# Statistics pass of a four-layer convolution kernel: scaling moved to GpSimd, loads into eight shared buffers

## The chip, the cores and the metric

The kernel runs on one core of a Trainium2 chip. The metric is the device time of one execution in microseconds (us); less is better. A core has five engines that run in parallel, each with its own queue of instructions: TensorE (PE in the profile), VectorE (DVE), ScalarE (ACT), GpSimd (POOL) and SyncE (SP, which here only issues DMA transfers). Engines wait for each other through semaphores.

## The reference

The input `x` has shape (4, 16, 512, 512). Four layers follow each other, each on all of it:

- layer 0: a depthwise 3x3 convolution, attention in windows of 8x8, and an MLP with GELU;
- layer 1: fake quantisation of the input and of the weights, a 3x3 convolution, a batch norm over the whole batch, and a clip to 0..6;
- layer 2: two 3x3 convolutions with a ReLU between them, and a residual;
- layer 3: a 3x3 convolution, a pointwise MLP of 128 hidden channels, and a residual.

What matters here is layer 1:

```python
def _fake_quant(v, n_bits, scaling_range):
    qp = float(2 ** (n_bits - 1) - 1)
    alpha = scaling_range * jnp.max(jnp.abs(v))
    step = alpha / qp
    q = jnp.clip(jnp.round(v / step), -qp, qp) * step
    return v + jax.lax.stop_gradient(q - v)

xq = _fake_quant(x, N_BITS_A, SCALE_RANGE_IN)
wq = _fake_quant(weight, N_BITS_W, 1.0)
y = conv(xq, wq)                        # 3x3, same size
mean = jnp.mean(y, axis=(0, 2, 3))
var = jnp.var(y, axis=(0, 2, 3))
inv = gamma * jax.lax.rsqrt(var + BN_EPS)
y = y * inv + (beta - mean * inv)
return jnp.clip(y, 0.0, ACT_THRES)
```

The mean and the variance run over the whole output of the convolution. They must be known before the first value of layer 1 can be finished.

## The kernel before

The program has three stages. The first, `window_attention`, computes layer 0 and writes its result to a DRAM buffer `x1` of 65 blocks, each of 128 partitions x 4 x 512 float32 values (1 MB). It also collects the largest absolute values in `peak`. The other two are in `conv_layers`: a **statistics pass**, which computes layer 1's convolution for its mean and variance only and keeps none of its values, and then the **layer pass**, which reads `x1` again and computes layers 1, 2 and 3 together in one long pipeline (the loop `for t in range(-2, M + 7)`).

The statistics pass takes one block per step, 64 steps (M is 64). Per step:

- `load` brings a block from `x1` into an SBUF tile `tx` by one DMA of 1 MB, issued by SP. The pass has four tiles, two of the tag "x" and two of the tag "o" in the pool `ld`, in turn. Each is written again once ScalarE has read it. `load` runs four steps ahead.
- `scaled` (L984) multiplies the tile by 1/step and adds the constant `ROUND`, in place, on VectorE: 128 partitions x 2048 float32 values. The addition rounds to integers.
- `rounded` (L987) takes the constant off again on ScalarE and writes bfloat16 into the inner columns of a tile of the ring `q` (three tiles, 514 columns wide, of which the two outer columns are zero). `scaled` and `rounded` run two steps ahead of the convolution.
- `_conv_turn` (L908) is called 24 times with four matmuls each: 96 matmuls of 32x32 weights on 512 columns, into four PSUM banks of 512 values. Odd and even steps use different sets of four banks.
- `bn_stats` (L1009) reads each of the four banks on VectorE and leaves six values a partition.

Ahead of the loop, `quant_step` finds the maximum over `peak`; a GpSimd instruction takes it over the partitions. Behind the loop, two more tiles (-2 and -1, for the rows outside the blocks) are loaded, scaled and rounded, `bn_aggr` (L1031) puts the statistics together, and some twenty instructions on one column turn them into `scale` and `shift`.

The order of PE's, VectorE's, ScalarE's and SP's instructions in `conv_layers` is the order of the program (`manual_schedule`). GpSimd's instructions are placed by the compiler's scheduler.

The layer pass has rings of its own for what goes from layer to layer: `z` (3 tiles), `h` (2), `x` (2), `xi` (3) and `y` (3). All are 128 x 4 x 514 float32 values, and all have zeros in their two outer columns, which `ring` (L947) writes on GpSimd. None of these five rings is used in the statistics pass.

Of the kernel before, what the change touches and what calls it, by code (L numbers as in the profile page):

```python
# [11 lines left out]
F32 = mybir.dt.float32  # L12
BF16 = mybir.dt.bfloat16
AF = mybir.ActivationFunctionType
ALU = mybir.AluOpType
# [8 lines left out]
B, C, H, W = 4, 16, 512, 512  # L24
P = 128
HR = H // 2
WP = W + 2
NS = 8
S = 4
M = H // S // 2  # L30
# [5 lines left out]
ROUND = 12582912.0  # L36
# [77 lines left out]
def conv_chain(ctx: ExitStack, tc: tile.TileContext, x, xw, mats, vecs, cqs, cws, hots, out):  # L114
# [32 lines left out]
    with tc.If(safe == 0):  # L147
        attention_block(tc, x, x1, m, v, peak)
    conv_layers(tc, x1, out, cw, cq, sw, m, v, peak)


# [700 lines left out]
def quant_step(nc, pool, out, columns, name):  # L852

    most = pool.tile([P, 1], F32, name=f"most_{name}")
    nc.vector.tensor_reduce(most, columns, AX.X, ALU.max, apply_absolute_value=True)
    every = pool.tile([P, 1], F32, name=f"every_{name}")
    nc.gpsimd.partition_all_reduce(every, most, P, bass_isa.ReduceOp.max)
    step = out.tile([P, 1], F32, name=f"step_{name}")
    nc.vector.tensor_scalar(step, every, 1.0 / QP, None, ALU.mult)
    inv = out.tile([P, 1], F32, name=f"inv_{name}")  # L860
    nc.vector.reciprocal(inv, step)
    return step, inv
# [21 lines left out]
def _load_pairs(nc, t, x1, mm):  # L884


    if mm < 0:
        nc.vector.memset(t[:, 0], 0.0)
        nc.sync.dma_start(t[:, 1:S], x1[M + mm, :, 0 : S - 1])
    elif mm < M:  # L890
        nc.sync.dma_start(t, x1[mm])
    else:
        nc.sync.dma_start(t[:, 0 : S - 1], x1[mm - M, :, 1:S])
        if mm == M:
            nc.sync.dma_start(t[:, S - 1], x1[M, :, S - 1])
        else:
            nc.vector.memset(t[:, S - 1], 0.0)


def _turns():  # L900

    return [(side, dx, i) for side in range(2) for dx in range(3) for i in range(4)]


def _conv_turn(nc, p, weights, src, side, dx, i):

    for j in range(4):
        nc.tensor.matmul(  # L908
            p[i][_quad(j)], weights[_quad(i), side, dx, :],
            src[side][_quad(i), j, dx : dx + W],  # L910
            start=side == 0 and dx == 0, stop=side == 1 and dx == 2,
        )
# [3 lines left out]
def conv_layers(ctx: ExitStack, tc, x1, out, cw, cq, sw, m, v, peak):  # L916
# [18 lines left out]
    nc = tc.nc  # L935
    ld = ctx.enter_context(tc.tile_pool(name="l3l", bufs=2))
    act = ctx.enter_context(tc.tile_pool(name="l3a", bufs=1))
# [2 lines left out]
    banks = [ps.tile([P, W], F32, name=f"tb{i}") for i in range(8)]  # L940
    conv_banks, hid_banks = banks[0:4], banks[4:8]

    def ring(name, n, dt=F32):
        tiles = []
        for i in range(n):
            t = act.tile([P, 4, WP], dt, name=f"{name}{i}")
            nc.gpsimd.memset(t[:, :, 0 : WP : WP - 1], 0.0)  # L947
            tiles.append(t)
        return lambda mm: tiles[mm % n]

    qs = ring("q", 3, BF16)
    zs, hs, xs, xi, ys = ring("z", 3), ring("h", 2), ring("x", 2), ring("xi", 3), ring("y", 3)

    edge_b1 = act.tile([P, 2], F32, name="edge_b1")
    nc.vector.tensor_scalar(edge_b1, v("edge"), v("l2_b1"), None, ALU.mult)
# [19 lines left out]

    loaded = {}

    def load(mm, tag="x"):
        loaded[mm] = ld.tile([P, S, W], F32, tag=tag, name=f"tx{mm}")
        _load_pairs(nc, loaded[mm], x1, mm)  # L980

    def scaled(mm, at=slice(0, S)):
        t = loaded[mm][:, at]
        nc.vector.tensor_scalar(t, t, ix, ROUND, ALU.mult, ALU.add)  # L984

    def rounded(mm, at=slice(0, S)):
        nc.scalar.activation(  # L987
            inner(qs(mm))[:, at], loaded[mm][:, at], AF.Identity, bias=unround
        )


    tags = ("x", "o")
    for mm in range(4):
        load(mm, tags[mm % 2])
    sx, ix = quant_step(nc, act, act, peak, "x")
    for mm in range(2):
        scaled(mm)
        rounded(mm)
    for mm in range(M):
        if mm + 4 <= M:  # L1000
            load(mm + 4, tags[mm % 2])
        if mm + 2 <= M:
            scaled(mm + 2)
            rounded(mm + 2)
        p = banks[4 * (mm % 2) : 4 * (mm % 2) + 4]
        for turn in _turns():
            _conv_turn(nc, p, cq, (qs(mm), qs(mm + 1)), *turn)
        for b in range(B):
            nc.vector.bn_stats(stats[:, mm * B + b, :], p[b])  # L1009
    for mm in (-2, -1):  # L1010
        load(mm)
        scaled(mm)
        rounded(mm)
# [11 lines left out]
    def mul(a, b, name):  # L1025
        t = act.tile([P, 1], F32, name=f"mul_{name}")
        nc.vector.tensor_tensor(t, a, b, ALU.mult)
        return t
# [9 lines left out]
    s = mul(sx, sw, "s")  # L1038
# [135 lines left out]
    for t in range(-2, M + 7):  # L1174
# [5 lines left out]
        mm = t - 4  # L1180
# [5 lines left out]
        mm = t - 3  # L1186
# [7 lines left out]
        mm = t - 1  # L1194
# [4 lines left out]
        mm = t  # L1199
# [135 lines left out]
```

## Time and profile before

| | us |
|---|---|
| runs | 6492.53, 6498.27, 6499.6 |
| median | 6498.27 |
| profiled execution | 6499.56 |
| its span, first to last instruction | 6497.8 |
| statistics pass, first to last block of statistics (L1009), starts | 3573.7 to 3804.7 |
| PE busy in the span | 6264.0 (96%) |
| ACT busy | 4179.7 (64%) |
| DVE busy | 3186.5 (49%) |
| POOL busy | 6.0 (0%) |

The profile is of one execution. In its 40 slices of equal length each digit is the busy share of a slice in tenths. "PEclk" is the clock that TensorE was granted, as a share of full speed. In the groups of instructions a line names the code line, engine, operation, what is written and read, and the count, and behind the bar the busy time in us, the mean of one in ns, and the idle time of the engine just before with what ended it. In the timeline a line begins with start and length in us, and the bracket is the idle time before it and what ended it. Times of instructions that overlap on an engine are counted once in busy times.

### The profile page before, as it was taken

How to read it: one execution, taken by the hardware profiler on the slowest of the kernel's cores; microseconds unless marked ns; L12 is line 12 of the kernel's file. 1: busy time of each engine (PE TensorE's matmuls, PEld its weight loads, DVE VectorE, ACT ScalarE, POOL GpSimd, SP SyncE). 2: the span in 40 equal slices, each digit the busy share in tenths (PEclk: the TensorE clock that was granted, in tenths of full speed). 3: DMA queues.
4: the chain of work that ended last, by engine and by line, in shares of the span. 5: the costliest groups of instructions: out<-in, count | busy, mean ns of one | idle time of the engine just before them, and what ended most of it. 6: DMA issues, size and time to landing. Idle time of an engine off the chain costs nothing. (4 is left out here: it accounts for less than half of the span.)

```text
span 6497.8 us, 317055 instructions
## 1 busy us (share of the span) xinstructions
PE 6264.0 (96%) x146976; PEld 3402.1 (52%) x146976; DVE 3186.5 (49%) x4640; ACT 4179.7 (64%) x5738; POOL 6.0 (0%) x26
## 2 busy tenths in 40 slices
PE   8999999999999999999997669999999999999999
PEld 5555555555555555555553335455555554555553
DVE  3444444444444444444443974544445554545554
ACT  5777777777777777777775544555555555555554
POOL 0000000000000000000000000000000000000000
PEclk9999999999999999999997879999999999999999
DMA  3333333333333333333322842222222222222221
GB/s 82 62 71 62 71 63 70 63 70 63 70 63 70 63 70 62 71 61 72 60 56 61 298 161 75 81 82 86 83 82 81 82 83 82 84 83 81 81 65 48
DMA packets 544390, 515.30 MB, mean 79 GB/s; under 512 B 349008, under 2 KB 480208, under 8 KB 514384
## 3 DMA queue, kind: packets, MB, share of 16 engines
q1 hardware_dynamic: 542768, 494.52, 29.2%
q8 instruction: 1154, 18.91, 1.2%
q14 instruction: 180, 1.47, 0.1%
q10 hardware_dynamic: 288, 0.39, 0.0%
HBM read 225.87 MB, written 134.48 MB: 55 GB/s over the span
## 5 line engine op out<-in xcount | busy, mean ns | idle before, releaser
L1123 ACT ACTIVATE hid<-tb,vec 128x512 f32<-128x512 f32 x1280 | 847.5, 687 | 1127.8 <-PE tb L1117 1126.5
L1117 PE MATMUL tb<-y,mat 32*32 32x512 f32 x16384 | 1567.9, 599 | 2.0 <-DVE o L1139 1.3
L367 ACT ACTIVATE e<-pair 128x1024 f32<-128x1024 f32 x1024 | 992.3, 1021 | 225.0 <-PE pair L359 224.3
L1125 DVE TENSOR_SCALAR hid<-tb,vec 128x512 f32<-128x512 f32 x768 | 575.3, 749 | 890.0 <-PE tb L1117 872.8
L295 PE MATMUL pair<-x,taps 32*32 32x512 f32 x18432 | 965.8, 605 | 1.9 <-ACT y L306 1.3
L416 PE MATMUL bank<-y,fc_e 32*32 32x512 f32 x8192 | 878.4, 607 | 3.7 <-ACT hid L421 3.2
L421 ACT ACTIVATE hid<-bank,f1b 128x512 f32<-128x512 f32 x1024 | 679.6, 686 | 298.8 <-PE bank L416 285.3
L351 DVE COPY yt<-bank 128x512 f32<-128x512 f32 x512 | 353.8, 691 | 906.1 <-PE bank L346 905.8
L359 PE MATMUL pair<-g,y 32*128 32x128 f32 x16384 | 651.2, 285 | 40.4 <-ACT e L367 39.3
L1117 PEld LDWEIGHTS tb<-y,mat 32*32 32x32 f32 x16384 | 496.4, 103 | 329.4 <-issue 185.0
L908 PE MATMUL tb<-z,cw 32*32 32x512 f32 x12864 | 640.4, 603 | 4.2 <-ACT z L1054 3.4
L359 PEld LDWEIGHTS pair<-g,y 32*128 32x128 f32 x16384 | 540.2, 186 | 186.8 <-ACT e L367 109.2
L908 PE MATMUL tb<-x,cw 32*32 32x512 f32 x12480 | 620.0, 597 | 1.5 <-ACT z L1054 1.5
L295 PEld LDWEIGHTS pair<-x,taps 32*32 32x32 f32 x18432 | 459.3, 103 | 286.3 <-issue 182.9
L908 PE MATMUL tb<-h,cw 32*32 32x512 f32 x12672 | 590.7, 601 | 1.8 <-ACT z L1054 1.5
L378 PE MATMUL bank<-e,yt 128*32 128x128 f32 x16384 | 555.3, 276 | 0.9 <-ACT r L393 0.9
L908 PE MATMUL tb<-q,cq 32*32 32x512 bf16 x12672 | 418.5, 424 | 138.4 <-ACT q L987 103.2
L383 PE MATMUL bank<-e,hot 128*32 128x512 f32 x4096 | 535.0, 593 | 0.0
L378 PEld LDWEIGHTS bank<-e,yt 128*32 128x32 f32 x16384 | 417.6, 109 | 108.1 <-DVE yt L351 52.8
L1133 PE MATMUL tb<-hid,mat 128*32 128x512 f32 x4096 | 471.1, 601 | 0.0
L429 DVE TENSOR_TENSOR xo<-bank,y 128x512 f32<-128x512 f32 x256 | 177.1, 692 | 547.2 <-PE bank L427 545.5
L346 PEld LDWEIGHTS bank<-mat,y 128*128 128x128 f32 x2048 | 215.3, 141 | 431.7 <-issue 378.1
(150 smaller groups left out, 6661.2 us busy)
## 6 DMA issues: line engine op xcount, KB each, us to landing
tx<-x SPq DMA_DIRECT2D x128, 1024.0 KB
x<-in_xw_dram SPq DMA_DIRECT2D x32, 2600.0 KB
y<-y SPq DMA_DIRECT2D x2048, 32.0 KB
xi<-x SPq DMA_DIRECT2D x1024, 64.0 KB
out_dram<-o SPq DMA_DIRECT2D x64, 1024.0 KB
x<-xo SPq DMA_DIRECT2D x2000, 32.0 KB
tx<-x SPq DMA_DIRECT2D x4, 768.0 KB
x<-xo SPq DMA_DIRECT2D x48, 24.0 KB
```

The lines of the kernel that those rows point to most:

```text
L295: nc.tensor.matmul(bank(u)[quad(vv)], taps[quad(u), tap, :], xts[n // 2][quad(u), vv, dy : dy + WS, at : at + BW], start=tap == 0, stop=ta ...
L359: nc.tensor.matmul(bank(u)[:, P * jj : P * jj + P], y2[quad(u), vv, jl + jj].rearrange("p w t -> p (w t)"), g[quad(u), vv, jl + jj].rearra ...
L367: nc.scalar.activation(e[:, 2 * i : 2 * i + 2].rearrange("p u j t -> p u (j t)"), pairs[i], AF.Exp,)
L378: nc.tensor.matmul(b[quad(u), P * jj : P * jj + P], yt[:, jj, quad(u)], e[:, u, jj, :], start=True, stop=True,)
L383: nc.tensor.matmul(d[quad(u)], own, e[:, u].rearrange("p j t -> p (j t)"), start=True, stop=True,)
L416: nc.tensor.matmul(b[quad(k)], fc1[quad(vv), quad(k)], y[quad(vv), u, :], start=True, stop=True,)
L421: nc.scalar.activation(hd, b, AF.Gelu, bias=f1b)
L908: nc.tensor.matmul(p[i][_quad(j)], weights[_quad(i), side, dx, :], src[side][_quad(i), j, dx : dx + W], start=side == 0 and dx == 0, stop= ...
L1117: nc.tensor.matmul(p[_quad(c)], w1[_quad(b), 1 - par, 32 * c : 32 * c + 32], inner(ys(mm + par))[_quad(b), s, :], start=True, stop=True,)
L1123: nc.scalar.activation(hd, p, AF.Relu, bias=v("l3_b1"))
L1125: nc.vector.tensor_scalar(hd, p, v("l3_b1"), 0.0, ALU.add, ALU.max)
L1133: nc.tensor.matmul(p[_quad(b), :], w2[:, par], hd, start=par == 0, stop=par == 1)
```

## The change

The loop's scalings go from VectorE to GpSimd (`scaled` takes an engine). The scalings of tiles 0 and 1, those of tiles -2 and -1, and those of the layer pass stay on VectorE. The pass's loads no longer use tiles of the pool `ld`. They go into the eight tiles of the rings `y`, `xi` and `x`, seen as flat rows of which the first 2048 of 2056 values are used. The loads run eight steps ahead, and a step's load stands behind its statistics in the program. The zeros in the outer columns of these three rings are written behind the loop, since the loads overwrite some of them; those of `q`, `z` and `h` stay where they were.

```diff
+    rings = {}
+
     def ring(name, n, dt=F32):
-        tiles = []
-        for i in range(n):
-            t = act.tile([P, 4, WP], dt, name=f"{name}{i}")
+        tiles = rings[name] = [
+            act.tile([P, 4, WP], dt, name=f"{name}{i}") for i in range(n)
+        ]
+        return lambda mm: tiles[mm % n]
+
+    def border(name):
+        for t in rings[name]:
             nc.gpsimd.memset(t[:, :, 0 : WP : WP - 1], 0.0)
-            tiles.append(t)
-        return lambda mm: tiles[mm % n]
 
     qs = ring("q", 3, BF16)
     zs, hs, xs, xi, ys = ring("z", 3), ring("h", 2), ring("x", 2), ring("xi", 3), ring("y", 3)
+    for name in "qzh":
+        border(name)
...
-    def load(mm, tag="x"):
-        loaded[mm] = ld.tile([P, S, W], F32, tag=tag, name=f"tx{mm}")
+    def load(mm, t=None):
+        if t is None:
+            t = ld.tile([P, S, W], F32, tag="x", name=f"tx{mm}")
+        loaded[mm] = t
         _load_pairs(nc, loaded[mm], x1, mm)
 
-    def scaled(mm, at=slice(0, S)):
+    def scaled(mm, at=slice(0, S), engine=nc.vector):
         t = loaded[mm][:, at]
-        nc.vector.tensor_scalar(t, t, ix, ROUND, ALU.mult, ALU.add)
+        engine.tensor_scalar(t, t, ix, ROUND, ALU.mult, ALU.add)
...
-    tags = ("x", "o")
-    for mm in range(4):
-        load(mm, tags[mm % 2])
+
+    flat = [
+        t.rearrange("p s x -> p (s x)")[:, 0 : S * W].rearrange("p (s x) -> p s x", x=W)
+        for t in rings["y"] + rings["xi"] + rings["x"]
+    ]
+    AHEAD = len(flat)
+    for mm in range(AHEAD):
+        load(mm, flat[mm])
     sx, ix = quant_step(nc, act, act, peak, "x")
     for mm in range(2):
         scaled(mm)
         rounded(mm)
     for mm in range(M):
-        if mm + 4 <= M:
-            load(mm + 4, tags[mm % 2])
         if mm + 2 <= M:
-            scaled(mm + 2)
+            scaled(mm + 2, engine=nc.gpsimd)
             rounded(mm + 2)
         p = banks[4 * (mm % 2) : 4 * (mm % 2) + 4]
         for turn in _turns():
             _conv_turn(nc, p, cq, (qs(mm), qs(mm + 1)), *turn)
         for b in range(B):
             nc.vector.bn_stats(stats[:, mm * B + b, :], p[b])
+        if mm + AHEAD <= M:
+            load(mm + AHEAD, flat[mm % AHEAD])
+    for name in ("x", "xi", "y"):
+        border(name)
```

## The prediction

> **What bounds the kernel now.** I read the page's 40 slices first. They show one short stretch unlike the rest: around slice 22 VectorE (DVE) and the DMA engines rise and TensorE (PE) falls.
>
> ```profile
> PE   8999999999999999999997669999999999999999
> DVE  3444444444444444444443974544445554545554
> POOL 0000000000000000000000000000000000000000
> DMA  3333333333333333333322842222222222222221
> ```
>
> That is the statistics pass. Everywhere else PE is the bound and the change touches nothing there, so the rest of the reading is of this pass. The table of windows gives its busy times (us, PE busy, PEld busy, DVE, ACT, POOL, PE clock, DMA share, GB/s):
>
> ```profile
> 3563.00:3566.00 3.00, 0.00 (x0) 0.00 (x0) 0.00 (x0) 0.00 (x0) 0.00 (x0) 0.50 0.90 371
> 3566.00:3569.00 3.00, 0.00 (x0) 0.00 (x0) 1.52 (x2) 1.25 (x1) 0.00 (x0) 0.50 1.04 437
> ...
> 3575.00:3800.00 225.00, 136.06 (x5952) 83.29 (x5936) 223.18 (x311) 122.98 (x62) 0.00 (x0) 0.83 0.80 288
> ```
>
> DVE is busy 223.18 of 225 us. No other engine is above 136, GpSimd (POOL) does nothing, and the loads run at 288 GB/s where the first ones reached 437. The groups of instructions inside this window say what DVE does:
>
> ```profile
> L1009 DVE BATCH_NORM_STATS2 stats<-tb 128x6 f32<-128x512 f32 x249 | 154.7, 682 | 1.8 <-PE tb L908 0.8
> L908 PE MATMUL tb<-q,cq 32*32 32x512 bf16 x5952 | 136.7, 459 | 88.9 <-ACT q L987 66.0 <-issue 22.1
> L987 ACT ACTIVATE q<-tx,unround 128x2048 bf16<-128x2048 f32 x62 | 124.3, 2005 | 102.4 <-DVE tx L984 72.3 <-PE tb L908 30.0
> L984 DVE TENSOR_SCALAR tx<-tx,inv_x 128x2048 f32<-128x2048 f32 x62 | 78.6, 1268 | 0.0
> ```
>
> Per step of the pass DVE does four statistics and one scaling, and never waits to speak of (1.8 us). ScalarE (ACT) waits for the scaling, PE waits for ACT: both are followers. The timeline of DVE shows the beat:
>
> ```profile
> 3692.88 1.27 DVE L984 TENSOR_SCALAR tx<-tx,inv_x 128x2048 f32<-128x2048 f32 x1
> 3694.07 2.48 DVE L1009 BATCH_NORM_STATS2 stats<-tb 128x6 f32<-128x512 f32 x4
> 3696.47 1.27 DVE L984 TENSOR_SCALAR tx<-tx,inv_x 128x2048 f32<-128x2048 f32 x1
> ```
>
> Start to start the scaling costs 3694.07 - 3692.88 = 1.19 us and the four statistics 3696.47 - 3694.07 = 2.40 us: 3.59 us a step. From the first group of statistics (3573.71) to the 64th (3802.87) there are 63 steps in 229.16 us, 3.637 us each. That is the figure to beat.
>
> [...] The trace of before has no elementwise GpSimd instruction with an input; it only has a fill:
>
> ```profile
> L279 POOL MEMSET y<- 128x4096 f32 x1 | 3.5, 3518 | 0.0
> ```
>
> 3518 ns for 4096 elements is 0.86 ns an element: [...]reading isn't shown. [...]
>
> **The change part by part.**
>
> 1. Off DVE: 63 scalings of 1.19 us each (those of tiles 0 and 1, before the loop, and the two after it stay). The DVE beat falls from 3.59 to 2.40 us. This is a gain only down to the next limit.
>
> 2. What is late next, per step. ACT's rounding: 2.00 us. PE: one timeline entry has 96 matmuls in 1.66 us at full clock; at half clock (right after the pass) 96 take 2.79 us. The clock was 0.83 on average at 60% busy[...]. Loads: 1.0486 MB at 437 GB/s is 2.40 us, and the first tiles landed 2.38 and 2.49 us apart:
>
> ```profile
> 3566.38 1.28 DVE L984 TENSOR_SCALAR tx<-tx,inv_x 128x2048 f32<-128x2048 f32 x1 [3.51 <-DMA tx<-x]
> 3568.76 1.29 DVE L984 TENSOR_SCALAR tx<-tx,inv_x 128x2048 f32<-128x2048 f32 x1 [1.09 <-DMA tx<-x]
> 3571.25 1.29 DVE L984 TENSOR_SCALAR tx<-tx,inv_x 128x2048 f32<-128x2048 f32 x1 [1.21 <-DMA tx<-x]
> ```
>
> So 2.44 us if the rate lasts. The other bound comes from the steady stretch: 288 GB/s at a share of 0.80 scales to 360 GB/s, or 2.91 us. I take 2.44, because a rate that demand sets (a load waits until ACT has freed one of four buffers) says little of the limit; 2.91 stays for the range.
>
> 3. On POOL: 63 scalings of 128x2048, the unknown of the case. [...] Below nothing isn't possible: POOL was idle. Behind a scaling on POOL's queue stand only later scalings and the border fills, so a wait for a load there holds up nothing else.
>
> 4. Eight buffers for four. A load into a buffer waits for ACT's rounding of the tile eight back, where it waited for four back. That takes the latency (the first load landed some 4.9 us after issue) off the loop of load, scaling, rounding. The three-engine chain is longer now, DMA to POOL to ACT to PE, and four buffers at 2.6 us a step would hold 10.4 us for some 4.9 + 2 + 2 us, so even four may have done. I put nothing on it by itself. The load in the program order now stands behind the step's statistics, but it is SP's instruction, in SP's own queue, and waits for ACT alone: its place costs nothing. The tiles for the two outer strips (-2, -1) are no longer behind the pass's buffers; before, DVE didn't wait for them either, so nothing.
>
> 5. Border fills. Eight of 16 fills (about 0.1 us each or less, on POOL) move from before the maximum over partitions to behind the last scaling. Before the pass they free 0.3 to 0.5 us of POOL, hidden by the first load (DVE waited 3.51 us for it). After the pass they wait for ACT's last roundings and take under 1 us on an idle POOL, with the statistics' aggregation (7.08 us on DVE) in front of anything that needs x, xi or y. Nothing. Uncovered, 0.8 us.
>
> 6. Once: [...]
>
> The sum: the floors are 2.40 (DVE), 2.44 (loads), 2.0 (ACT), 1.66 to 2.79 (PE). With three of them so close they will disturb each other; I take 2.60 a step. 63 x (3.637 - 2.60) = 65.3 us. Less 5 us for the fill of the longer chain and for stretches of PE at half clock: 60. The profiled execution took 6499.56 us (span 6497.8 and 1.76 around it), so 6439.5; the median of the runs lies 1.3 lower: 6438 us.
>
> **Rivals.**
>
> POOL or the loads at a middling rate. [...]Loads at 2.91: 63 x 0.727 = 46, less 3, so 6455. [...]
>
> Slower: POOL is the bound above the old beat. [...] It decides from 3.64 us a scaling, and is slower beyond the bound from 3.84. Eight buffers would not help, since the rate and not the latency limits. For it: no instruction of this sort is in the trace. [...]
>
> No change: POOL between 3.43 and 3.84 us, which returns what DVE loses.
>
> That the change doesn't do what it says: the order of DVE's instructions in the changed kernel has statistics back to back behind the first two scalings, and POOL has the scalings, so it does.
>
> **How the numbers follow.** Forecast (POOL under 2.9 a step, loads fast) 0.50, own range 6424 (2.44 a step without losses: 63 x 1.197 = 75) to 6455. Middling 0.24, 6455 to 6485. No change 0.06, slower 0.20. I call faster or slower what differs by over 0.2%, 13 us, which is about what a measurement of this kernel can tell from no change. So 0.74, 0.06, 0.20. The range for 8 in 10 holds the forecast, the middling rival and part of no change: 6424 to 6500.
>
> **What would show it.** Right: DVE in the pass without scalings and the beat of the statistics 2.4 to 2.9 us; POOL busy 50 to 100% there; DMA above 380 GB/s. Part 2 is wrong if PE stays at half clock with 2.8 us a step. Part 3 is wrong if POOL is busy without gaps and ACT waits for it at 3.2 us or more. Part 6 is wrong if the first POOL scaling starts well after 3572. Anything past the pass should keep its length.

## The result and the profile after

| | before | after |
|---|---|---|
| median of 20 runs, us | 6494.14 | 6510.93 |
| ratio, 95% interval | | 1.0025 [1.0019, 1.0032] |
| profiled execution (span), us | 6499.56 (6497.8) | 6504.77 (6503.0) |
| first statistics to aggregation, starts, us | 3573.7 to 3809.0 | 3572.4 to 3821.8 |
| a step of the pass, us | 3.638 | 3.862 |

The kernel became slower by 16.8 us, where 60 us less were forecast. The pass grew by 249.4 - 235.3 = 14.1 us in the two profiled executions, which is most of it; between separate executions some microseconds elsewhere differ too (the two spans differ by 5.2 us only). A step is the mean over 63 steps: the last start of a statistics instruction less the first, less 1.8 us for the three that precede the last one in its step (1.2 us for two in the run before3, 3.0 us for five in paced).

The same 40 slices of the page after:

```profile
PE   8999999999999999999997569999999999999999
DVE  3444444444444444444443664544554444554454
POOL 0000000000000000000000510000000000000000
DMA  3333333333333333333322732222222222222221
```

VectorE is down to 6 tenths in slices 22 and 23 (counted from 0), GpSimd has work, but TensorE and the DMA engines are a little lower than before, not higher. The table of windows after (us, PE busy, PEld busy, DVE, ACT, POOL, PE clock, DMA share, GB/s):

```profile
3563.00:3566.00 3.00, 0.00 (x0) 0.00 (x0) 0.88 (x1) 0.00 (x0) 0.00 (x0) 0.50 1.00 412
3566.00:3569.00 3.00, 0.45 (x30) 0.28 (x32) 1.70 (x2) 2.13 (x2) 0.00 (x0) 0.50 1.01 401
...
3575.00:3800.00 225.00, 133.51 (x5470) 89.52 (x5470) 139.48 (x226) 117.11 (x59) 122.56 (x66) 0.76 0.76 289
```

No engine is full any more: the busiest, VectorE, has 139 of 225 us. The loads run at 289 GB/s, where before had 288. So something else holds every engine back. The groups of instructions in this window:

```profile
L1020 DVE BATCH_NORM_STATS2 stats<-tb 128x6 f32<-128x512 f32 x226 | 139.6, 684 | 85.6 <-PE tb L908 85.2
L908 PE MATMUL tb<-q,cq 32*32 32x512 bf16 x5470 | 133.7, 513 | 92.8 <-issue 86.9 <-ACT q L995 3.4 <-DVE stats L1020 2.2
L992 POOL TENSOR_SCALAR xi<-xi,inv_x 128x2048 f32<-128x2048 f32 x24 | 47.3, 1973 | 39.0 <-DMA xi<-x 39.0
L995 ACT ACTIVATE q<-xi,unround 128x2048 bf16<-128x2048 f32 x23 | 46.0, 2006 | 53.0 <-PE tb L908 53.0
```

Read the part behind the second bar as a chain. GpSimd (1.97 us a scaling) waits for loads, ScalarE and VectorE wait for PE, and a load waits until ScalarE has read its buffer (SyncE, which issues the loads, waited 186.9 us for ScalarE here). PE itself was idle 92.8 us, of which 86.9 are put down to "issue": it waited for no other engine. The same group had 22.1 us of "issue" before. The timeline of PE after shows what these gaps are:

```profile
3637.80 3.70 PE L908 MATMUL tb<-q,cq 32*32 32x512 bf16 x128 [4.05 <-issue]
3644.01 3.19 PE L908 MATMUL tb<-q,cq 32*32 32x512 bf16 x128 [2.51 <-issue]
3648.86 3.27 PE L908 MATMUL tb<-q,cq 32*32 32x512 bf16 x128 [1.66 <-issue]
...
3658.26 3.62 PE L908 MATMUL tb<-q,cq 32*32 32x512 bf16 x128 [1.18 <-issue]
3663.66 2.08 PE L908 MATMUL tb<-q,cq 32*32 32x512 bf16 x128 [1.77 <-issue]
3668.50 3.71 PE L908 MATMUL tb<-q,cq 32*32 32x512 bf16 x128 [2.76 <-issue]
```

A step has 96 matmuls, but PE runs 128 at a time and then stops. 128 matmuls with their weight loads are 256 instructions. The DMA view has a queue "instruction". For the whole of before it has (packets, MB, share of 16 engines):

```profile
q8 instruction: 1154, 18.91, 1.2%
```

That is 16.4 KB a packet. PE has 146976 matmuls and as many weight loads in the span, so 254.7 of its instructions a packet and 64.3 bytes an instruction: the queue fits PE's instructions alone. Between 3600 and 3700 us of the changed kernel:

```profile
q8 instruction: 19, 0.31, 1.2%
```

In these 100 us PE ran 100 / 3.862 x 192 = 4972 instructions, or 19.4 times 256. So I read a packet as a **page** of 256 of PE's instructions, and PE's stops as waits for the next page.

The trace has start and length of each of these packets, and they agree with that. Six of the bursts above stand behind packets that ended at 3636.55, 3642.74, 3647.39, 3656.81, 3662.35 and 3667.17 us: PE resumes 1.25 to 1.47 us after each. Of the 41 packets that start between 3585 and 3800 us, 39 are followed by such a start of PE out of a gap of over 0.25 us, 1.24 to 1.62 us after their end. The next packet starts 2.40 us after the end of the last at the soonest, so when PE has already begun on that one: in this stretch no two pages are on their way at a time. A packet takes 0.96 us (median) with loads beside it or without; what differs is the time from the end of one to the start of the next, a median of 4.18 us here and 2.54 us in the run noload below, which has no loads in that stretch.

The timeline of PE before had the marks of it:

```profile
3646.96 0.82 PE L908 MATMUL tb<-q,cq 32*32 32x512 bf16 x34 [0.41 <-issue]
3649.03 1.62 PE L908 MATMUL tb<-q,cq 32*32 32x512 bf16 x94 [1.25 <-ACT q L987]
3652.07 0.39 PE L908 MATMUL tb<-q,cq 32*32 32x512 bf16 x2 [1.42 <-issue]
```

34 + 94 is 128, with an "issue" gap in front of the 34 and another behind the 94. There the gaps lay where PE had to wait for ScalarE soon after anyway, because VectorE's 3.59 us a step left room.

### The profile page after: what moved, and what is told of

It reads as the page before. It is cut to its first block, busy times and chain, and to the rows that moved or that the text cites. A ratio compares the mean times of both kernels' runs of the same rounds, so it can differ in the third digit from the quotient of the medians.

```text
span 6503.0 us, 316992 instructions
## 1 busy us (share of the span) xinstructions
PE 6258.7 (96%) x146976; PEld 3412.4 (52%) x146976; DVE 3114.6 (48%) x4577; ACT 4176.7 (64%) x5738; POOL 130.8 (2%) x89
## 3 DMA queue, kind: packets, MB, share of 16 engines
q14 instruction: 179, 1.47, 0.1%
```

## The experiments

A page lasts a step's time x 128 / matmuls in a step. The ratio in the last column is to executions of before on the same chip; a dash means a single execution, whose step is read from its trace. Scaling "none" means that the loop has no scalings; where only a part of the loads is named, the loop leaves out the others. The edits are shown shortened.

| run | scaling | buffers | loads | matmuls | step, us | page, us | time / before [95%] |
|---|---|---|---|---|---|---|---|
| before | VectorE | 4 | all | 96 | 3.638 | 4.85 | 1 |
| after | GpSimd | 8 | all | 96 | 3.862 | 5.15 | 1.0025 [1.0019, 1.0032] |
| pool4 | GpSimd | 4 | all | 96 | 3.833 | 5.11 | 1.0033 [1.0021, 1.0045] |
| dve8 | VectorE | 8 | all | 96 | 3.725 | 4.97 | 1.0008 [1.0002, 1.0015] |
| noload | GpSimd | 8 | first 8 | 96 | 2.863 | 3.82 | - |
| quarter | GpSimd | 8 | a quarter | 96 | 3.057 | 4.08 | - |
| third | GpSimd | 8 | all | 32 | 2.541 | 10.2 | - |
| before3 | VectorE | 4 | all | 96 | 3.661 | 4.88 | - |
| split4 | GpSimd | 8 | in 4 pieces | 96 | 4.071 | 5.43 | 1.0049 [1.0032, 1.0065] |
| blk64 | GpSimd | 8 | all | 48 (64x64) | 2.629 | 7.01 | 0.9911 [0.9894, 0.9927] |
| blk64c | GpSimd | 8 | all | 96 (64x64) | 3.686 | 4.91 | - |
| blk64d4 | GpSimd | 4 | all | 48 (64x64) | 2.903 | 7.74 | 0.9932 [0.9919, 0.9946] |
| before64 | VectorE | 4 | all | 48 (64x64) | 3.590 | 9.57 | 0.9997 [0.999, 1.0003] |
| paced | GpSimd | 4 | all | 96 | 3.985 | 5.31 | 1.003 [1.0017, 1.0042] |
| nopool8 | none | 8 | all | 96 | 3.833 | 5.11 | - |
| nopool4 | none | 4 | all | 96 | 3.960 | 5.28 | - |
| nothing | none | 8 | first 8 | 96 | 2.789 | 3.72 | - |

**Parts of the change alone: pool4 and dve8.**

```diff
-    AHEAD = len(flat)
+    AHEAD = 4                                # pool4
```
```diff
-            scaled(mm + 2, engine=nc.gpsimd)
+            scaled(mm + 2)                   # dve8
```

> As the changed kernel, but only four of the eight buffers are used (loads run four steps ahead). Theory F (the loads queued on the DMA engines hold up TensorE's own instruction pages, 128 matmuls with their weight loads each): fewer loads in flight, pages come sooner; the idle time of PE put down to 'issue' between 3575 and 3800 falls from 87 us towards the 22 us of before, the pass takes 2.8 to 3.4 us a step instead of 3.86, and the kernel is 25 to 60 us faster than the changed one, so 10 to 45 us faster than before. Rival L (the loads themselves are late, since GpSimd waits 97 us for them): half the buffers make it worse or leave it at 3.86 or more a step. Rival C (TensorE at half clock sets the step): unchanged, 3.8.

> As the changed kernel, but the scaling is back on VectorE: eight buffers alone. Theory F: the deep queue of loads starves TensorE here too; about 3.8 to 3.9 us a step, VectorE waits for TensorE in the pass, slower than before by 10 to 20 us. If the deep buffers are harmless and the loss comes from GpSimd: 3.59 to 3.64 us a step with VectorE busy throughout, the time of before within 5 us.

pool4: 6512.72 us, 3.83 us a step. What theory F expected, 2.8 to 3.4 us a step and a faster kernel, did not come: half the buffers don't bring the pages sooner, and 3.83 is near what rivals L and C gave. The next two runs decide between the three. For theory F it leaves that the loads' total rate, not their number in the queue, may be what counts. dve8: 6500.28 us, 3.725 us a step, between the two expectations. Eight buffers by themselves cost 0.09 us a step; most of the loss comes with the other half of the change, the scaling on GpSimd.

**Loads taken away, instructions taken away: noload and third.**

```diff
-            load(mm + AHEAD, flat[mm % AHEAD])
+            loaded[mm + AHEAD] = flat[mm % AHEAD]     # noload
```
```diff
-        for turn in _turns():                         # third
-            _conv_turn(nc, p, cq, (qs(mm), qs(mm + 1)), *turn)
+        for side in range(2):
+            for i in range(4):
+                for j in range(4):
+                    nc.tensor.matmul(
+                        p[i][_quad(j)], cq[_quad(i), side, 1, :],
+                        qs(mm + side)[_quad(i), j, 1 : 1 + W],
+                        start=side == 0, stop=side == 1,
+                    )
```

> As the changed kernel, but the pass loads only its first eight blocks and scales and rounds those again (the other loads are left out, and from step 8 on the scaling multiplies by another number of the same shape). Theory F: nothing competes with TensorE's instruction pages; 2.45 to 2.7 us a step (VectorE's four statistics of 2.40 us are the bound), gaps of PE put down to 'issue' nearly gone. If pages come too slowly by themselves, whatever the loads do: about 3.8 us a step with the same gaps after 128 matmuls. Rival C: 2.8 us.

> As the changed kernel, but the statistics pass does only the middle one of three column shifts: 32 matmuls a step instead of 96, all loads kept. Theory F: a step needs a third of the instructions, so pages of 128 matmuls last four steps; 2.45 to 2.9 us a step, bound by the statistics (2.40) or the loads (2.44). Rival L (the loads are the bound): stays at 3.8 us a step. Rival C falls here too, so this run tells F and C from L only.

third takes 2.54 us a step with every load. The window from 3575 to 3700 us of third:

```profile
3575.00:3700.00 125.00, 76.18 (x1616) 18.88 (x1608) 122.95 (x202) 99.95 (x51) 97.99 (x51) 0.50 1.01 420
```

The loads run at 420 GB/s and a DMA share of 1.01, although PE is at half clock throughout (0.50). So the loads (rival L) don't hold the changed kernel at 3.86. noload takes 2.86 us a step, not the 2.45 that VectorE would allow, and its timeline of PE still stops at every page:

```profile
3643.44 2.20 PE L908 MATMUL tb<-q,cq 32*32 32x512 bf16 x128 [0.63 <-issue]
3647.18 2.07 PE L908 MATMUL tb<-q,cq 32*32 32x512 bf16 x128 [1.55 <-issue]
```

Start to start that is 3.74 us, and PE stops although it runs a page in 2.1 to 2.2 us, with a clock of 0.97 from 3575 to 3700 us; so half clock (rival C) isn't the cause. A page takes 3.8 us with no loads at all and 5.15 us among them: theory F is right about the direction of the loads, but about three quarters of a page's time are there without them, which it had not expected (2.45 to 2.7 us a step).

**Dose, and the pieces of a load: quarter and split4.**

```diff
+            if mm + AHEAD < M:                        # quarter, on noload
+                nc.sync.dma_start(flat[mm % AHEAD][:, 0:1], x1[mm + AHEAD][:, 0:1])
```
```diff
-        nc.sync.dma_start(t, x1[mm])                  # split4
+        for i in range(4):
+            nc.sync.dma_start(t[:, i : i + 1], x1[mm][:, i : i + 1])
```

> As the changed kernel, but from the ninth block on only a quarter of each block is loaded (256 KB; the last load is left out), the rest of the tile is worked on again. Theory F: between none (2.86 us a step) and all of the loads (3.86): 3.0 to 3.3 us. If pages are slow by themselves and loads don't matter: 3.8.

> As the changed kernel, but each of the pass's loads is issued as four DMAs of 256 KB (one of four rows each). Theory P, a form of F: a page waits behind the piece of a load that its DMA engine has begun; smaller pieces, shorter waits: pages of 4.0 to 4.6 us, 3.0 to 3.5 us a step, 20 to 50 us faster than the changed kernel. If a page gets its share of the engine by bytes whatever the pieces: 3.7 to 3.9 us a step as now.

quarter lies between, 4.08 us a page at 108 GB/s. In split4 only the pass's loads are split. That smaller pieces would let a page in sooner was a guess. They didn't: 5.43 us a page, and 6525.49 us. Theory P falls in this form. The DMA share also rose (0.92 from 3575 to 3700 us, against 0.81 in the changed kernel there), so this run doesn't say what would happen at an equal load. At which place the loads hold a page up is open.

**The limit was there before: before3.**

```diff
-        for b in range(B):
-            nc.vector.bn_stats(stats[:, mm * B + b, :], p[b])
+        for b in range(3):
+            nc.vector.bn_stats(stats[:, mm * 3 + b, :], p[b])
```

> The kernel before with its scaling on VectorE and its four buffers, but only three of the four banks go through the statistics (the fourth is left out): VectorE's step falls by 0.60 us without GpSimd. Theory F: 2.99 us a step isn't reached, since pages come every 4.5 to 5.2 us under loads; 3.4 to 3.9 us a step, gaps of PE after 128 matmuls as in the changed kernel. If the loss lies with GpSimd or the deep buffers: 3.0 us a step, some 40 us faster than before.

With 0.60 us less on VectorE, and nothing else changed in the loop, a step takes 3.66 us instead of 3.64. The groups from 3575 to 3700 us of this run:

```profile
L908 PE MATMUL tb<-q,cq 32*32 32x512 bf16 x3360 | 75.0, 464 | 54.1 <-issue 32.5 <-ACT q L987 21.3
...
L1009 DVE BATCH_NORM_STATS2 stats<-tb 128x6 f32<-128x512 f32 x105 | 66.1, 685 | 19.4 <-PE tb L908 18.8
```

VectorE now waits for PE, and PE for its pages in 32.5 of 54.1 us; for the rest it waits for ScalarE, whose tile VectorE scales behind the statistics. So the kernel before had no slack under VectorE to give: VectorE's 3.59 us a step and PE's pages (4.88 us here, or 3.66 a step) were two limits at almost the same place. Relieving one buys nothing.

**Fewer instructions for the same work: blk64, blk64c.** The convolution of the pass with 64x64 weights, two copies of the 32x32 block on the diagonal, needs half the matmuls (the largest form that the page of before lists for PE's tiles is 128*128: 64*64 is a quarter of it, 32*32 a sixteenth):

```diff
+    cq2 = act.tile([P, 2, 3, 64], BF16, name="cq2")
+    nc.vector.memset(cq2, 0.0)
+    for i in range(4):
+        at = 32 * (i % 2)
+        nc.vector.tensor_copy(cq2[_quad(i), :, :, at : at + 32], cq[_quad(i)])
...
-        for turn in _turns():
-            _conv_turn(nc, p, cq, (qs(mm), qs(mm + 1)), *turn)
+        for side in range(2):
+            for dx in range(3):
+                for jj in range(2):
+                    for h in range(2):
+                        for g in range(2):
+                            half, out64 = slice(64 * h, 64 * h + 64), slice(64 * g, 64 * g + 64)
+                            nc.tensor.matmul(
+                                p[2 * h + jj][out64], cq2[half, side, dx, :],
+                                qs(mm + side)[half, 2 * jj + g, dx : dx + W],
+                                start=side == 0 and dx == 0, stop=side == 1 and dx == 2,
+                            )
```

blk64c has a loop over the two halves of 256 columns outside of these, so that there are 96 matmuls again.

> As the changed kernel, all loads and the whole computation kept, but the statistics pass's convolution works with block-diagonal 64x64 weights: 48 matmuls a step instead of 96, each on a quarter of the array instead of a sixteenth. Theory F (TensorE's instruction pages of 128 matmuls set the step, 3.86 x 128 / 96 = 5.15 us a page): a page now lasts 2.67 steps, 1.93 us a step, so the array itself becomes the bound, 12 groups of four at 0.21 to 0.28 us, 2.6 to 3.4 us a step; gaps of PE put down to 'issue' nearly gone; 25 to 65 us faster than before. Rival C (half clock): twice the array time, over 5 us a step, slower than the changed kernel by 80 us. Rival L (loads): 3.8 us a step as now.

> As blk64 (GpSimd scaling, eight buffers), but each matmul split into two of 256 columns: the array's work is that of blk64, the number of TensorE's instructions is again that of the changed kernel (96 matmuls and 96 weight loads a step). Theory F: the pages count, so again 128 matmuls and a gap put down to 'issue', 5.1 to 5.6 us a page, 3.8 to 4.2 us a step. If it was the size or shape of the matmuls on the array that held the changed kernel up: 2.6 to 2.9 us a step.

blk64: 6435.26 us, 0.9911 [0.9894, 0.9927] of before. The window of blk64:

```profile
3575.00:3700.00 125.00, 123.11 (x2264) 93.18 (x2260) 116.20 (x187) 96.04 (x48) 97.30 (x50) 0.99 1.01 420
```

Loads (420 GB/s), PE (123 of 125 us) and VectorE (116) are all nearly full. Four of these matmuls take 123.11 x 4 / 2264 = 0.218 us. The instruction queue brought 14 packets between 3600 and 3700 us: 100 / 2.629 x 96 / 256 = 14.3. blk64c has the array's work of blk64 and the instructions of the changed kernel, and is back at 3.69 us a step with this timeline of PE:

```profile
3627.61 5.36 PE L1029 MATMUL tb<-q,cq 64*64 64x256 bf16 x128 [2.24 <-issue]
3633.27 3.70 PE L1029 MATMUL tb<-q,cq 64*64 64x256 bf16 x128 [0.30 <-issue]
3639.21 3.70 PE L1029 MATMUL tb<-q,cq 64*64 64x256 bf16 x128 [2.24 <-issue]
```

That is a little under the 3.8 to 4.2 expected, with the stops where expected. It is the number of PE's instructions, and not the matmuls' size, that holds the pass.

**What each half is worth once pages don't bind: blk64d4 and before64** (AHEAD = 4 on blk64; the 64x64 loop on the kernel before).

> As blk64 (GpSimd scaling, 48 matmuls of 64x64 a step), with four of the eight buffers. If the deep buffers matter once TensorE's pages don't: the chain load, scaling, rounding of some 5 + 2 + 2 us and the wait in the load queue over four buffers, 2.7 to 3.1 us a step against 2.63, 5 to 30 us slower than blk64. If the loads' rate alone sets it: 2.63 as with eight, the same time within 10 us.

> The kernel before (scaling on VectorE, its four buffers) with the 48 matmuls of 64x64 a step. Theory F: VectorE's 3.59 us a step stays the bound, TensorE's gaps go; 3.59 to 3.62 us a step instead of 3.638, at most 5 us faster than before. So the gain of blk64 needs both edits. If the 64x64 matmuls alone bring it: 2.7 us a step, 60 us faster.

before64 is the same as before within the interval: VectorE's 3.59 us is then the only limit, to the hundredth. blk64d4 takes 2.90 us a step and 6453.99 us: eight buffers are worth 0.27 us a step there. So both halves are worth something once PE's pages are out of the way.

**Why slower and not the same: paced, nopool8, nopool4, nothing.** Two limits at one place explain no gain, but not the further 0.2 us a step.

```diff
             nc.vector.bn_stats(stats[:, mm * B + b, :], p[b])
+            if b < 2:                                 # paced, on pool4
+                nc.vector.bn_stats(again[:, b, :], p[b])
```
```diff
-            scaled(mm + 2, engine=nc.gpsimd)          # nopool8; nopool4 on pool4; nothing on noload
```

> As pool4 (GpSimd scaling, four of the eight buffers), with two of the four statistics of each step done a second time into a spare tile: VectorE works 2.40 + 2 x 0.60 = 3.60 us a step again, as before the change, while GpSimd still scales. If VectorE's even beat in the kernel before kept the loads apart from TensorE's pages (and without it, loads and pages bunch): more work, yet 3.60 to 3.68 us a step instead of 3.83, 8 to 15 us faster than pool4. If GpSimd's scaling by itself, or the longer chain over it, costs the pages: 3.83 or more, no faster than pool4.

> The changed kernel without the loop's 63 scalings (left out, on any engine); loads into eight buffers, rounding, matmuls and statistics stay. If GpSimd's work slows the pages: under 3.7 us a step instead of 3.86. If the loads and TensorE alone make the step: 3.80 to 3.95.

> As nopool8 with four buffers, against pool4 (3.83 us a step). If GpSimd's work slows the pages: about 3.6 us. If the release of loads by TensorE's beat does: 3.75 to 3.9 us.

> As noload (loads left out from the ninth block on), also without the loop's scalings: only rounding, matmuls and statistics. If GpSimd's work slows the pages: 2.45 to 2.7 us a step instead of 2.86. If pages take some 3.8 us with nothing beside them: 2.8 to 2.9 us.

GpSimd's work isn't the cause: without any scaling the step is 3.83 (nopool8) and 3.96 us (nopool4) with loads, and 2.79 against 2.86 without. Less work than before, and a slower pass. Giving VectorE its 3.60 us a step back (paced) didn't help either, it made 4.0, where 3.60 to 3.68 would have spoken for VectorE's beat. The run isn't clean: between 3580 and 3800 us PE waited 11.1 us for the longer statistics, some 0.2 us a step. What differs in the DMA view from 3600 to 3780 us is how even the loads are; before, and then the changed kernel:

```profile
DMA  8887788778877888788787878788888777888888
```
```profile
DMA  9976783894669668865966985987795876497389
```

In before VectorE's scaling stands in the chain that frees a buffer, once a beat. After, ScalarE's rounding waits for PE, PE runs a page of 1.33 steps and stops, and buffers come free and loads start in the same rhythm as the pages. That loads and pages then meet more often is a likely reason. Uneven loads alone are not, for before3, at 3.66 us a step, has them too:

```profile
DMA  9559983979967799869599956889668986589857
```

What tells the runs apart is where the busy stretches lie. Take the 2 us after a page has let PE resume (1.4 to 3.4 us after its packet ended), from 3585 to 3800 us. There the loads fill 0.87 of the DMA engines' time in the changed kernel and 0.88 to 0.94 in pool4, nopool8, nopool4 and paced, against 0.71 to 0.76 over the whole stretch. In before, before3, dve8 and blk64c they fill 0.71 to 0.76 there, against 0.75 to 0.79 over the whole. From the end of one page's packet to the start of the next the mean is 4.2 to 4.4 us in the first five and 3.7 to 3.9 us in the other four. So pages and loads do meet more often in the slower runs. That this makes the difference is not shown: within the changed kernel the wait hardly follows the share (correlation 0.26), and no run changes the meeting alone.

## Why the prediction was wrong

- **The failed step is part 2, "What is late next".** It priced PE by how long the array takes (1.66 to 2.79 us for 96 matmuls) and not by how fast PE gets its instructions. Those come at 4.9 to 5.2 us for 128 matmuls beside the loads, 3.7 to 3.9 us a step. The sum took 2.60 as a step; 3.86 was measured. The evidence was in the quoted line of PE ("issue 22.1") and in its bursts, which I read as PE following ScalarE; and the quoted line of ScalarE had it waiting 30.0 us for PE, which a mere follower doesn't cause.
- Part 1 was right in itself: VectorE is left with the statistics, and in the changed kernel eight of them in a row take 4.88 us, 2.44 for four.
- The loads of part 2 were right: 420 GB/s in third and blk64. The clock between 3575 and 3800 us was 0.76, where before had 0.83, but it isn't what set the step: noload has 0.97 and still stops at every page, third has 0.50 and takes 2.54 us a step.
- Part 3: 1.97 us a scaling, so GpSimd wasn't the bound (122.56 of 225 us busy). The trace of before has no multiply and add on GpSimd, so what the prediction put on each speed of it was its author's estimate. The two rivals with a slow GpSimd fell with it, and so did the mechanism given for "slower". The chance of 0.20 for "slower" came true by a mechanism that the prediction didn't have, which is luck.
- Part 4 put nothing on the eight buffers. Beside slow pages they cost a little (dve8, 3.725 against 3.638 us); with pages out of the way they bring 0.27 us a step.
- Part 5 was right: the border fills don't show. Part 6 was wrong by the prediction's own mark of 3572 us: GpSimd's first scaling started at 3573.08, 2.9 us after its tile could be used:

```profile
3573.08 1.96 POOL L992 TENSOR_SCALAR y<-y,inv_x 128x2048 f32<-128x2048 f32 x1 [11.93 <-issue]
...
3577.13 3.25 PE L908 MATMUL tb<-q,cq 32*32 32x512 bf16 x126 [3.40 <-ACT q L995]
```

The profile names no cause for the 11.93 us, but most of it is the load: the tile's last packet ended at 3569.61 us, and the last semaphore record of GpSimd's queue before the scaling (17 ns) ended at 3570.22. The other 2.9 us lay behind the load. What GpSimd did in them isn't shown. PE then waited 3.40 us. The second group of statistics starts 6.2 us after the first instead of 3.6: 2.6 us, once. They are in the mean step of 3.862; from the second group on it is 3.82.

## What to carry to other kernels

Before you relieve the busiest engine of a stage, look at the second limit in that stage, and count instructions as well as their durations: TensorE was held here by how fast its many short instructions came, which showed as idle time put down to "issue" after every 128 matmuls, 86.9 of 225 us. A stage can sit on two limits at once, and then one edit shows nothing and only both together do (before64: nothing, after: a loss, blk64: 0.9% faster). The test is to take a little work off the first limit and look whether the step follows.

## What the runs showed of the hardware that was not expected

- TensorE's instructions came in packets of 16.4 KB, 254.7 instructions each over the whole of before, and in the changed kernel TensorE stopped after every 128 matmuls with their weight loads. The packet of the next page started there only after PE had begun on the last (2.40 us or more after that one's packet had ended). A page took 3.7 to 3.8 us in runs without loads, 4.1 beside loads at 108 GB/s and 4.9 to 5.4 beside loads of 267 to 323 GB/s. In blk64, with loads at 420 GB/s, one was needed every 7.0 us and came in time: from 3575 to 3700 us PE waited 1.9 us, and that for ScalarE.
- 128 matmuls of 32x32 with their weight loads ran in 2.07 us in noload, at a clock of 0.97, where a page took 3.82 us.
- GpSimd's multiply and add of 128x2048 float32 took 1.97 us, 0.96 ns an element, and its spread over 63 of them was 1957 to 1994 ns beside VectorE's statistics. These took 684 ns in the mean there, and 682 ns in before with no work on GpSimd. That is no sign that the two block each other.
